# A two-layer graph network with seven-product matmuls: an output sum in halves, two output products set between the relational ones, and a new order in the fill and the first turn

## The chip, the cores and the metric

The kernel runs on one core of a Trainium2 chip. A core has five engines with instruction streams of their own: TensorE (PE) for matmuls and transpositions, VectorE (DVE), ScalarE (ACT), GpSimd (POOL) and SyncE (SP), which here only issues transfers. The metric is the device time of one execution in microseconds (us), the median of several runs. Everything is computed in 32-bit floats.

## The reference, cut to what matters

64 graphs of 256 nodes with 256 features each go through two layers. Layer 0 is a graph attention (GAT) twice, a norm, a feed-forward with ReLU (256 to 1024 and back), and a norm. Layer 1 is a relational attention with 8 heads and 4 relations, a norm, a feed-forward with GELU, and a norm.

```python
def _gat(h, adj, W, a, out_features):
    Wh = h @ W                                    # 256 -> 256
    e = leaky_relu(Wh @ a[:out] + swapaxes(Wh @ a[out:], 1, 2), 0.2)
    att = softmax(where(adj > 0, e, NEG), axis=1)
    return att @ Wh
# layer 0
h = _gat(_gat(x, adj, W1, a1), adj, W2, a2)
h = _layernorm(x + h, g_ln1, b_ln1)
x = _layernorm(h + relu(h @ w_ff1 + b_ff1) @ w_ff2 + b_ff2, g_ln2, b_ln2)
# layer 1
q, k = heads(x @ Wq + bq), heads(x @ Wk + bk)     # 8 heads of 32
attn = softmax(q @ k.T / sqrt(32))
out = sum(attn * (adj == r) @ heads(x @ Wv[r] + bv[r]) for r in range(4))
x = _ln(x + out @ Wo + bo, g1, beta1)
return _ln(x + gelu(x @ W1 + b1) @ W2 + b2, g2, beta2)
```

## The kernel before

**Groups and turns.** The 64 graphs are cut into 32 groups (`NG`) of two; a group is T = 4 blocks of 128 nodes, two to a graph. A fill (L539 to L567 and L1694 to L1853) brings in the weights and does all of layer 0 for group 0 but its end, and the two GATs of group 1. Then come 32 calls of `turn(y_, x_, z)`. A turn works on three groups at once: layer 1 of group y_, the feed-forward of layer 0 of group x_ = y_ + 1, and both GATs of group z = y_ + 2. The first 30 turns have a group z (in the code: `if Z`). In their order a turn has: the projections q and v of the relational attention and the first product of layer 0's feed-forward; the scores, exponentials, masks and weighted sums of the 8 heads; then the stretch that the change touches in every turn: the product with Wo (`out_(0)` and `out_(1)`, one for each graph), the second product of layer 0's feed-forward, between its parts the GAT of group z; then layer 1's feed-forward.

**Products in seven.** The large products are computed as two by two blocks with 7 products instead of 8 (Strassen and Winograd's form), so the inputs of some products are sums or differences of quarters, formed on DVE. `HiddenOut` (L1016) is the second product of a feed-forward. Its four sums take the quarters of the hidden layer `h`: sums 1 and 2 go into a tile called `eq` in the profile, sums 3 and 4 into `eaq`:

```python
o, x_, y_, op = ((s1, a21, a22, ALU.add), (s2, s1, a11, ALU.subtract),
                 (s3, a11, a21, ALU.subtract), (s4, a12, s2, ALU.subtract))[n - 1]
```

A sum is one instruction over 128 x 1024 elements. A product is 8 matmuls, which are 16 records in the profile. Products 1 and 2 read `h` (`yf<-wf,h`), 5 and 6 read sums 1 and 2 (`yf<-wf2t,eq`), 3 and 7 read sums 4 and 3 (`yf<-wf,eaq`), 4 reads `h`. `add(n)` adds what a product has left in its PSUM bank to the rows y. Products 1, 2 and 5 start in banks of their own; 6, 7 and 4 go on in the bank of 1, and 3 in that of 5, each after the add of the product before it there. `out(1)` is `product(1)` and then `add(1)`. The differences of weights that the form needs (`w2t` for layer 1's second product; `wvm`, `w1m`, `w2m` in the code) are formed once, on POOL, by `made(ops, n)`, n instructions a call (L631).

**Banks.** Most products write into a ring of six PSUM banks (`bank(...)`): a product can start when the bank's reader of before has ended. So a late reader on DVE or ACT holds PE.

**The order.** In the fill the order of all engines is that of the code. In the turns PE, SP, DVE and ACT follow the code in the first part and PE and SP in all of it; the rest is ordered by a planner. `with behind(mark)` puts an instruction behind another.

**The stretch in the middle of a turn.** In a turn with a group z its order before is this (L1507 to L1600):

```python
out.sums(1)                      # DVE, eq
shares(1)                        # DVE: zo transposed (L1174), division of po
out_(0)                          # PE: yop, then DVE: the add to y
mv = moments(y_, 2, y, range(NB))
out.sums(2)                      # DVE, eq
out_(1)
...
out(1)                           # PE: product 1, DVE: add 1
```

After it come the scores of the GAT (L819 is its leaky ReLU, on DVE), sum 4, `offsets` (DVE, `nm`, L896), products 2 and 5, and then 6, 3 and 7, with the `hpp` matmuls of the GAT's first sums between them. `norm` is moments on DVE and two instructions on POOL (`rs`, L888 and L889); `offsets` and `applied_norm` need its result.

**The fill.** `gat_weights` transposes the GAT's weights and the first x; `to_features` (L536) copies the two transposed banks of x, one on ACT and one on DVE. After the weights' small products (`gwep`) the adjacency of group 0 is squared on ACT as a check of its values (`checked`), copied and transposed on PE (`aTp`, L755), and then `project(0, [0, 1])` makes the products `xpp` (L773).

**The first projections.** The first turn starts with the end of the fill: `rest()` is `second_half` (L1848). There the second half of group 0's rows is transposed into `h2T`, whose two parts are copied from their banks. `Projections` (L1065) then makes q and v in steps 1 to 7, with four differences on DVE (`p.sums()`), and copies each bank of q on ACT (L1101) and adds v's on DVE.

Of the kernel before, what the change touches and what calls it, by code (L numbers as in the profile page):

```python
# [16 lines left out]
P = 128  # L17
# [368 lines left out]
def narrow_path(  # L386
# [152 lines left out]
    def gat_weights():  # L539

        w1s = work.tile([P, KB, F], F32, tag="hT", name="gw1")
        nc.scalar.dma_start(w1s, g_W1.rearrange("(c p) f -> p c f", p=P))
        w2e = work.tile([P, KB, WX], F32, tag="wh", name="gw2e")
        nc.sync.dma_start(w2e[:, :, :F], g_W2.rearrange("(c p) f -> p c f", p=P))
        load_first(0)
        gcols = columns([v.rearrange("f o -> (f o)") for v in (g_a1, g_a2)], "ga", nc.scalar, "yt")

        def transposed(w, name):
            wt = work.tile([P, KB, F], F32, tag="e", name=f"{name}t")
            for c in range(KB):  # L550
                ps = bank(f"{name}tp{c}")
                for k in range(KB):
                    nc.tensor.transpose(ps[:, k * P:(k + 1) * P], w[:, k, c * P:(c + 1) * P], ident)
                nc.vector.tensor_copy(wt[:, c, :], ps[:, :F])
            return wt

        w1t, w2t = transposed(w1s, "gw1"), transposed(w2e, "gw2")
        a1, a2 = gcols()
        g[0]["xT"] = to_features(g[0]["y"], "xT0")
        for k in range(KB):  # L560
            ps = bank(f"gwap{k}")
            for c in range(KB):
# [150 lines left out]
    def normed_features(u, l, xn, natural=False, copied=(), later=False):  # L713
# [17 lines left out]
        for q in range(Q):  # L731
            for a in range(Q):
                to, at = hT[q * 32:(q + 1) * 32, a], yt[a * 32:(a + 1) * 32, q]
                if q == a:
                    nc.gpsimd.tensor_copy(to, at)  # L735
                else:
                    if n not in copied:
                        nc.sync.dma_start(to, at)
                    elif later:
                        moves.append((to, at))  # L740
                    else:
                        nc.scalar.copy(to, at)
                    n += 1
# [272 lines left out]
    class HiddenOut:  # L1016
# [6 lines left out]
            s.a = [h1[:, k * K2:(k + 1) * K2, b * N:(b + 1) * N] for b in range(2) for k in range(2)]  # L1023
            s.ps = {}

        def sums(s, *which):
            a11, a12, a21, a22 = s.a
            s1, s2, s3, s4 = s.s
            for n in which:
                o, x_, y_, op = ((s1, a21, a22, ALU.add), (s2, s1, a11, ALU.subtract),  # L1030
                                 (s3, a11, a21, ALU.subtract), (s4, a12, s2, ALU.subtract))[n - 1]
                mark["quarters"] = nc.vector.tensor_tensor(o, x_, y_, op)  # L1032

        def product(s, n):
            b11, b21, b22, t1, t2, t3, t4 = s.w
            K2, F2 = FB // 2, F // 2
            if n in (1, 2, 5):
                s.ps[n] = bank(f"yf{n}_{s.n}")
            for old, new in ((1, 6), (6, 7), (7, 4), (5, 3)):
                if n == new:  # L1040
                    s.ps[n] = s.ps[old]
            a, w_ = {1: (s.a[0], b11), 2: (s.a[1], b21), 5: (s.s[0], t1), 6: (s.s[1], t2),
                     3: (s.s[3], b22), 7: (s.s[2], t3), 4: (s.a[3], t4)}[n]
            for i in range(NB):
                for k in range(K2):
                    nc.tensor.matmul(s.ps[n][:, i * F2:(i + 1) * F2], a[:, k, i * P:(i + 1) * P], w_[:, k, :],  # L1046
                                     start=n in (1, 2, 5) and i == 0 and k == 0, stop=True,
                                     skip_group_check=True)
# [16 lines left out]
    class Projections:  # L1065
# [7 lines left out]
            s.h = [[hT[k][:, b * N:(b + 1) * N] for b in range(G)] for k in range(KB)]  # L1073
            s.one, s.two, s.begun, s.t = {}, {}, set(), [None] * 4

        def sums(s):
            tt = work.tile([P, HPB, NB * N], F32, tag="e", name=f"tq{s.u}").rearrange("p a n -> p (a n)")
            s.t = [tt[:, n * N:(n + 1) * N] for n in range(4)]
            for n, (x_, y_) in enumerate(((s.h[0][1], s.h[0][0]), (s.h[1][1], s.t[0]),
                                          (s.h[1][1], s.h[0][1]), (s.h[1][0], s.t[1]))):  # L1080
                nc.vector.tensor_tensor(s.t[n], x_, y_, ALU.subtract)

        def out(s, x, o, b):
            if x == "q":
# [240 lines left out]
    def turn(y_, x_, z, rest=None):  # L1325
# [49 lines left out]
        with order:  # L1375
            if not y_:
                p("q1 v1")
                rest()
                p("q2 v2")
            p.sums()  # L1380
            if X:
                n = X.pop("n")
                if y_:
                    offsets(*n)
                if y_:
                    p("q2 v2 q1 v1")
                else:
                    offsets(*n)
                applied_norm(X["y"], *n, [0, 1, 2, 3])
                p("q5")  # L1390
            else:
# [9 lines left out]
                w, wy = waiting[0]  # L1401
                last = moments(w, 3, wy, range(NB))
            if X:
                moved(moves, 2)
                p("q6")
                moved(moves, 1)
                p("v6")
                moved(moves, 3)
                times(X["y"], rg1)
                p("q3 q7 v7")  # L1410
# [96 lines left out]
            if X:  # L1507
                out = HiddenOut(x_, 0, X["y"], X["h1"], wf2s, out_sums(x_, 0))
                if Z:
                    out.sums(1)  # L1510
            if Z:
                shares(1)
            if not y_:
                with behind("low"):
                    made(w1m, 2)
                    made(w2m, 4)
            out_(0)
            if Z:
                mv = moments(y_, 2, y, range(NB))
# [1 line left out]
                n = norm(y_, 2, y, range(NB))  # L1521
            piece()
            if Z:
                out.sums(2)
            elif X:
                out.sums(1)
                out(1, 2)
# [9 lines left out]
                applied_norm(y, *n)  # L1537
                n = norm(y_, 2, y, range(NB, T))
            if Z:
                out(1)  # L1540
                Z["m"].scores(0)
                Z["m"].scores(1)
                Z["m"].exp(0)
# [31 lines left out]
            if Z:  # L1575
                out.product(6)
                hT = normed_features(y_, 2, y, copied=(1, 2, 4, 5, 7, 8, 10, 11))
                nc.scalar.activation(work.tile([P, 1], F32, tag="ve", name=f"ve{y_}"), mhalf[:, 0:1], AF.Gelu)
                out.add(6)
                out.sums(3)  # L1580
# [113 lines left out]
    with tc.manual_schedule(engines={getattr(mybir.EngineType, n) for n in  # L1694
# [202 lines left out]
```

## Time and profile before

| | |
|---|---|
| median of 3 runs | 2943.12 us (2942.83 to 2954.23) |
| the profiled execution | 2942.66 us |
| its span in the profile | 2941.0 us |
| TensorE clock granted, mean | 0.998 |
| PE busy | 2913.7 us (99%) |
| DVE busy | 2631.4 us (89%) |
| ACT busy | 1907.9 us (65%) |
| POOL busy | 707.9 us (24%) |
| from yop to yop, in the middle of the run | 89.77 us |

The span is the time from the first to the last instruction in the trace of one execution. A line of a timeline gives start, duration, engine, line of the code, operation, output<-input, shape and count, and in brackets an idle time before it with what ended it. The ends of matmuls are modelled, so that the duration of a group of matmuls is longer than the distance to the start of the next group. A group of a page's fifth part has the busy time, the mean of one in ns, and the idle time before.

### The profile page before, as it was taken

Reading aid. Unit: us, or ns where it says so; the run is one execution under the profiler, and the core shown is the slowest. Engines: PE = TensorE matmul, PEld = TensorE weight load, DVE = VectorE, ACT = ScalarE, POOL = GpSimd, SP = SyncE. Lnnn points to the kernel's source line nnn. Section 1 sums busy time; section 2 is a strip of 40 time slices with the busy share of each in tenths; the row PEclk is TensorE's granted clock in tenths of the full one; section 3 lists DMA queues with packets and bytes.
Section 4 is the critical chain, followed back from the end, with each engine's and each line's share of the span. In section 5 each row is a group of like instructions: output and inputs, shape, how many; then the busy total and the mean of one; then the engine's idle time right before and its main releaser. Section 6 shows DMA issues by size and latency. Waiting matters only on the chain.

```text
span 2941.0 us, 58470 instructions
## 1 busy us (share of the span) xinstructions
PE 2913.7 (99%) x21966; PEld 2477.7 (84%) x21966; DVE 2631.4 (89%) x5087; ACT 1907.9 (65%) x3985; POOL 707.9 (24%) x931
## 2 busy tenths in 40 slices
PE   9999999999999999999999999999999999999998
PEld 7788888888888888888888888888888888888876
DVE  5889999899989999999999899999999998999987
ACT  5576676676666766766766666667667666666653
POOL 3322221222221222212222212222122222222210
PEclk9999999999999999999999999999999999999999
DMA  5011211111111212111111111121112121121000
GB/s 153 15 36 40 44 37 34 38 42 41 42 36 27 43 40 44 38 34 37 43 40 42 36 27 43 40 44 37 36 35 43 39 44 35 28 42 40 24 10 16
DMA packets 417860, 115.11 MB, mean 39 GB/s; under 512 B 359994, under 2 KB 409380, under 8 KB 417572
## 3 DMA queue, kind: packets, MB, share of 16 engines
q1 hardware_dynamic: 416172, 109.98, 16.5%
q8 instruction: 176, 2.88, 0.4%
q0 software_dynamic: 1056, 1.05, 0.1%
q14 instruction: 112, 0.92, 0.1%
q10 hardware_dynamic: 344, 0.28, 0.0%
HBM read 72.51 MB, written 16.90 MB: 30 GB/s over the span
## 4 chain that ended last, share of the span: by engine, by line
PE 96%; DVE 2%; ACT 1%; POOL 1%; DMA 0%; issue 0%; POOLq 0%; DVEq 0%; ACTq 0%
PE yf L1046 27%; PE h1a L954 15%; PE h1b L954 12%; PE po L1163 8%; PE v L1114 6%; PE qk L1114 6%; PE sp L1135 4%; PE hpp L851 4%; PE ygp L862 4%; PE xpp L773 4%; PE yop L862 4%; PE zo L1166 2%; DMA first<-in_adj_dram 0%; ACT h L972 0%; POOL w2t L631 0%
## 5 line engine op out<-in xcount | busy, mean ns | idle before, releaser
L1144 ACT ACTIVATE e<-sp 128x512 f32<-128x512 f32 x512 | 270.9, 612 | 71.2 <-issue 43.7
L1148 DVE TENSOR_TENSOR ea<-e,aT 128x1024 f32<-128x1024 f32 x256 | 310.7, 1215 | 1.6 <-ACT e L1144 1.6
L963 DVE TENSOR_TENSOR h<-h1a,h 128x512 f32<-128x512 f32 x293 | 201.7, 689 | 90.3 <-PE h1a L954 89.1
L906 ACT ACTIVATE y<-y,nm,rs 128x256 f32<-128x256 f32 x442 | 235.0, 591 | 58.1 <-DVE nm L896 57.4
L735 POOL COPY hT<-yt 32x256 f32<-32x256 f32 x244 | 211.4, 866 | 144.7 <-PE v L1114 90.9
L966 ACT COPY h<-h1b 128x512 f32<-128x512 f32 x293 | 175.4, 599 | 109.0 <-PE h1b L954 107.2
L888 POOL TENSOR_SCALAR rs<-mv 128x4 f32<-128x4 f32 (+1 forms) x134 | 41.2, 307 | 794.6 <-DVE mv L878 625.4
L972 ACT ACTIVATE h<-h,cols 128x256 f32<-128x256 f32 x512 | 226.1, 504 | 9.8 <-DVE h L963 9.6
L1101 ACT COPY qk<-qk 128x512 f32<-128x512 f32 x128 | 74.3, 580 | 232.5 <-PE qk L1114 230.0
L1176 POOL TENSOR_TENSOR low<-low,rq 128x16 f32<-128x16 f32 x64 | 13.9, 217 | 844.0 <-DVE rq L1175 836.2
L877 DVE BATCH_NORM_STATS2 st<-y 128x6 f32<-128x256 f32 x512 | 208.3, 408 | 4.6
L972 ACT ACTIVATE h<-h1a,cols 128x256 f32<-128x256 f32 x256 | 103.0, 467 | 142.3 <-PE h1a L954 142.2
L1054 DVE TENSOR_TENSOR y<-yf,y 128x256 f32<-128x256 f32 x448 | 182.3, 407 | 11.3 <-PE yf L1046 11.3
L918 DVE TENSOR_TENSOR y<-y,rb 128x1024 f32<-128x1024 f32 x126 | 163.3, 1296 | 3.2
L727 POOL COPY hT<-yt 32x256 f32<-32x256 f32 x120 | 124.9, 1041 | 145.2 <-PE h1a L954 136.2
L1153 DVE TENSOR_TENSOR es<-e 128x1024 f32<-128x1024 f32 x128 | 155.6, 1216 | 0.0
L915 DVE TENSOR_TENSOR y<-y,rg 128x1024 f32<-128x1024 f32 x126 | 152.8, 1213 | 0.0
L889 POOL TENSOR_TENSOR rs<-rs,mhalf 128x4 f32<-128x4 f32 (+1 forms) x134 | 148.2, 1106 | 8.3
L822 ACT ACTIVATE s<-s 128x512 f32<-128x512 f32 x128 | 76.4, 627 | 109.8 <-DVE s L819 109.4
L1135 PE MATMUL sp<-qk 32*128 32x256 f32 x2048 | 138.4, 394 | 0.0
L954 PE MATMUL h1a<-tt,wf 128*128 128x256 f32 x512 | 137.7, 392 | 0.0
L1046 PEld LDWEIGHTS yf<-wf,eaq 128*128 128x128 f32 x1024 | 120.2, 193 | 20.3 <-DVE eaq L1032 11.9
(290 smaller groups left out, 7849.0 us busy)
## 6 DMA issues: line engine op xcount, KB each, us to landing
hT<-yt SPq DMA_DIRECT2D x666, 32.0 KB, 1.9
y<-in_x_dram SPq DMA_DIRECT2D x32, 512.0 KB, 4.3
xq<-in_x_dram SPq DMA_DIRECT2D x240, 64.0 KB, 2.1
aq<-in_adj_dram SPq DMA_DIRECT2D x240, 64.0 KB, 2.3
rows<-line SPq DMA_DIRECT2D x60, 256.0 KB, 3.2
out_dram<-y SPq DMA_DIRECT2D x30, 512.0 KB, 2.8
wf<-in_L_gnn_w_ff_dram SPq DMA_DIRECT2D x2, 1024.0 KB, 8.3
w<-in_L_gnn_W_dram SPq DMA_DIRECT2D x2, 1024.0 KB
```

What stands on the lines that cost most here:

```text
L735: nc.gpsimd.tensor_copy(to, at)
L862: nc.tensor.matmul(ps[:, i * F:(i + 1) * F], lhs(t, k), rhs(b, k), start=(k == 0), stop=(k == n - 1))
L877: nc.vector.bn_stats(st[:, t, :], y[:, t, :])
L906: mark["normed"] = nc.scalar.activation(y[:, t, :], y[:, t, :], AF.Identity, bias=nm[:, t:t + 1], scale=rs[:, t:t + 1])
L954: nc.tensor.matmul(ps[:, i * N:(i + 1) * N], w_[:, f * P:(f + 1) * P], m, start=first and i == 0, stop=True, skip_group_check=True)
L972: nc.scalar.activation(y, y if ps is None else ps[:, i * N:(i + 1) * N], func, bias=bi[:, f:f + 1])
L1046: nc.tensor.matmul(s.ps[n][:, i * F2:(i + 1) * F2], a[:, k, i * P:(i + 1) * P], w_[:, k, :], start=n in (1, 2, 5) and i == 0 and k == 0, s ...
L1114: nc.tensor.matmul(ps[:, i * N:(i + 1) * N], l, r, start=n in (1, 2, 5) and i == 0, stop=True, skip_group_check=True)
L1135: nc.tensor.matmul(ps[a][:, j * N:(j + 1) * N], k_[hp, m, j0:j0 + P], q[hp, m, b * N:(b + 1) * N], start=True, stop=True)
L1144: nc.scalar.activation(e[:, a, :], ps[a], AF.Exp, scale=isd)
L1148: nc.vector.tensor_tensor(ea[:, a:a + 2, :], e[:, a:a + 2, :], ab[:, None, :].to_broadcast([P, 2, NB * N]), ALU.mult)
L1163: nc.tensor.matmul(po[hp, m * N:(m + 1) * N], vs[:, hp], w[:, a, j * N:(j + 1) * N], start=(n == 0), stop=(n == len(terms) - 1))
```

## The change

- In the fill both copies of the first transposed x are on DVE; `project(0, [0, 1])` stands before the check of the adjacency and its transposition.
- In group 0's first output, sum 4 and products 2 and 5 stand before the GAT's scores and exponentials; products 3 and 7 and the norm stand before `made(wvm, 4)`, POOL's differences of the v weights.
- `second_half` transposes first, copies one part on DVE and one on ACT, takes the first difference of the projections, sets the row of ones on DVE instead of POOL, and only then takes the rest of the moments and the norm; `offsets` stands before the other three differences. In the first turn the copy of q6 stands before two moves on ACT, not behind them.
- In the first turn two of the four differences `w2m` are put behind the copies of the transposed y in POOL's order (`mark["turned"]`), not in front of them.
- In all turns with a group z, sum 2 is formed in two halves, the first before `shares(1)`, the second where the whole stood; and the first two of the eight matmuls of product 1 stand between `out_(0)` and `out_(1)`.

```diff
@@ gat_weights
-        g[0]["xT"] = to_features(g[0]["y"], "xT0")
+        g[0]["xT"] = to_features(g[0]["y"], "xT0", (nc.vector.tensor_copy,) * 2)
@@ normed_features
-                    nc.gpsimd.tensor_copy(to, at)
+                    mark["turned"] = nc.gpsimd.tensor_copy(to, at)
@@ HiddenOut
-        def sums(s, *which):
-            a11, a12, a21, a22 = s.a
-            s1, s2, s3, s4 = s.s
+        def sums(s, *which, half=None):
+            K2 = FB // 2
+            part = slice(0, K2) if half is None else slice(half * K2 // 2, (half + 1) * K2 // 2)
+            a11, a12, a21, a22 = [a[:, part] for a in s.a]
+            s1, s2, s3, s4 = [a[:, part] for a in s.s]
...
-        def product(s, n):
+        def product(s, n, some=None):
...
-            if n in (1, 2, 5):
+            if n in (1, 2, 5) and n not in s.ps:
                 s.ps[n] = bank(f"yf{n}_{s.n}")
...
-            for i in range(NB):
-                for k in range(K2):
-                    nc.tensor.matmul(...)
+            steps = [(i, k) for i in range(NB) for k in range(K2)]
+            for i, k in steps if some is None else steps[some]:
+                nc.tensor.matmul(...)
@@ Projections
-        def sums(s):
+        def sums(s, which=range(4)):
...
-                nc.vector.tensor_tensor(s.t[n], x_, y_, ALU.subtract)
+                if n in which:
+                    nc.vector.tensor_tensor(s.t[n], x_, y_, ALU.subtract)
@@ turn
             if not y_:
                 p("q1 v1")
-                rest()
+                rest(lambda: p.sums([0]))
                 p("q2 v2")
-            p.sums()
+                offsets(*X["n"])
+                p.sums([1, 2, 3])
+            else:
+                p.sums()
...
             if X:
-                moved(moves, 2)
+                if y_:
+                    moved(moves, 2)
                 p("q6")
-                moved(moves, 1)
+                moved(moves, 1 if y_ else 2)
                 p("v6")
+                if not y_:
+                    moved(moves, 1)
                 moved(moves, 3)
...
                 if Z:
                     out.sums(1)
+                    out.sums(2, half=0)
             if Z:
                 shares(1)
             if not y_:
                 with behind("low"):
                     made(w1m, 2)
-                    made(w2m, 4)
+                    made(w2m, 2)
             out_(0)
...
             if Z:
-                out.sums(2)
+                out.sums(2, half=1)
+                out.product(1, slice(0, 2))
...
             out_(1)
...
             if Z:
-                out(1)
+                out.product(1, slice(2, None))
+                out.add(1)
...
             if Z:
                 out.product(6)
                 hT = normed_features(y_, 2, y, copied=(1, 2, 4, 5, 7, 8, 10, 11))
+                if not y_:
+                    with behind("turned"):
+                        made(w2m, 2)
@@ fill
+        project(0, [0, 1])
         checked(0, g[0]["aq"], squares[:, 2:4].rearrange("p a n -> p (a n)"))
         turn_a = early_adjacency_of(0, 0)
         turn_a()
-        project(0, [0, 1])
...
         first.sums(1)
         first(1)
         first.sums(2)
+        first.sums(4)
+        first(2, 5)
         spread(b["m"])
         powers(b["m"])
-        first.sums(4)
-        first(2, 5)
         b["m"].masks(0)
...
+        first(3)
+        first(7)
+        n0 = norm(0, 1, a["y"], range(NB))
         made(wvm, 4)
-        first(3)
-        n0 = norm(0, 1, a["y"], range(NB))
-        first(7)
...
             nc.scalar.copy(h2T[:, 1, ns], ph[1][:, ns])
             nc.gpsimd.memset(h2T[one, KB - 1, ns], 1.0)
-            (nc.scalar.copy, nc.vector.tensor_copy)[b_](h2T[:, 0, ns], ph[0][:, ns])
+            nc.scalar.copy(h2T[:, 0, ns], ph[0][:, ns])
...
-        def second_half():
+        def second_half(first_difference):
+            turned(a["y"], "h2T0", range(NB, T), ph)
+            ns = slice(N, 2 * N)
+            nc.vector.tensor_copy(h2T[:, 0, ns], ph[0][:, ns])
+            nc.scalar.copy(h2T[:, 1, ns], ph[1][:, ns])
+            first_difference()
+            nc.vector.memset(h2T[one, KB - 1, ns], 1.0)
             b["n"] = norm(1, 0, b["y"], mv=mv)
-            turned(a["y"], "h2T0", range(NB, T), ph)
-            half(1)
```

More of the change, by code (lines that the diff above doesn't have):

```diff
@@ L1043, in product @@
                      3: (s.s[3], b22), 7: (s.s[2], t3), 4: (s.a[3], t4)}[n]
-            for i in range(NB):
-                for k in range(K2):
-                    nc.tensor.matmul(s.ps[n][:, i * F2:(i + 1) * F2], a[:, k, i * P:(i + 1) * P], w_[:, k, :],
-                                     start=n in (1, 2, 5) and i == 0 and k == 0, stop=True,
-                                     skip_group_check=True)
+            steps = [(i, k) for i in range(NB) for k in range(K2)]
+            for i, k in steps if some is None else steps[some]:
+                nc.tensor.matmul(s.ps[n][:, i * F2:(i + 1) * F2], a[:, k, i * P:(i + 1) * P], w_[:, k, :],
+                                 start=n in (1, 2, 5) and i == 0 and k == 0, stop=True,
+                                 skip_group_check=True)
         def add(s, n):
@@ L1074, in __init__ @@
             s.one, s.two, s.begun, s.t = {}, {}, set(), [None] * 4
-        def sums(s):
-            tt = work.tile([P, HPB, NB * N], F32, tag="e", name=f"tq{s.u}").rearrange("p a n -> p (a n)")
-            s.t = [tt[:, n * N:(n + 1) * N] for n in range(4)]
+        def sums(s, which=range(4)):
+            if which[0] == 0:
+                tt = work.tile([P, HPB, NB * N], F32, tag="e", name=f"tq{s.u}").rearrange("p a n -> p (a n)")
+                s.t = [tt[:, n * N:(n + 1) * N] for n in range(4)]
             for n, (x_, y_) in enumerate(((s.h[0][1], s.h[0][0]), (s.h[1][1], s.t[0]),
                                           (s.h[1][1], s.h[0][1]), (s.h[1][0], s.t[1]))):
-                nc.vector.tensor_tensor(s.t[n], x_, y_, ALU.subtract)
+                if n in which:
+                    nc.vector.tensor_tensor(s.t[n], x_, y_, ALU.subtract)
         def out(s, x, o, b):
@@ L1386, in turn @@
                     p("q2 v2 q1 v1")
-                else:
-                    offsets(*n)
                 applied_norm(X["y"], *n, [0, 1, 2, 3])
```

## The prediction

> **What bounds the kernel now.** I read the page first, then the waits of the PE, then the timelines of PE, DVE, ACT and POOL in four places (fill, first projections, end of the first turn, end of a later turn), then the windows with the granted clock. The busy line of the page, and the two longest lines of the waits of the PE:
>
> ```profile
> PE 2913.7 (99%) x21966; PEld 2477.7 (84%) x21966; DVE 2631.4 (89%) x5087; ACT 1907.9 (65%) x3985; POOL 707.9 (24%) x931
> ...
> PE yf L1046 <- DVE y L1054: 4.5, 6, 2.6
> PE aTp L755 <- ACT xT L536: 3.8, 1, 3.8
> ```
>
> PE sets the time, and idles only 27 us of 2941. But busy is not fast: a wait that is shorter than the tail of the matmul before it shows no idle time, only a later start. So I read starts. Timeline of the PE at the end of the sixth turn (start, duration, ..., count):
>
> ```profile
> 583.28 3.75 PE L862 MATMUL yop<-wo,qk 128*128 128x256 f32 x16
> 586.88 3.73 PE L1046 MATMUL yf<-wf,h 128*128 128x128 f32 x32
> 590.45 3.74 PE L1046 MATMUL yf<-wf2t,eq 128*128 128x128 f32 x32
> 594.15 2.05 PE L1046 MATMUL yf<-wf,eaq 128*128 128x128 f32 x16
> 596.04 1.91 PE L851 MATMUL hpp<-xp,s 128*128 128x258 f32 x8
> 597.95 2.05 PE L1046 MATMUL yf<-wf,eaq 128*128 128x128 f32 x16
> 599.84 1.91 PE L851 MATMUL hpp<-xp,s 128*128 128x258 f32 x8
> ```
>
> Start to start, undisturbed: 32 yf take 3.57 (586.88 to 590.45), so 16 take 1.79; 8 hpp take 1.74 (599.84 to 601.58), and 8 ygp in the fill 1.73, so 16 yop should take 3.46. Seen: yop 3.60 (0.14 over), products 5 and 6 3.70 (0.13 over, the wait of product 3), product 3 1.89 (0.10), hpp 1.91 (0.17, the wait of product 7), product 7 1.89 (0.10). That is 0.64 us a turn, in 29 like turns after the first 18.6 us. Who is late is seen in the DVE's timeline:
>
> ```profile
> 580.60 1.18 DVE L1032 TENSOR_TENSOR eq<-h 128x1024 f32<-128x1024 f32 x1
> 582.45 0.72 DVE L1174 STREAM_TRANSPOSE rz<-zo 128x512 f32<-128x512 f32 x1 [0.67 <-PE zo L1166]
> ...
> 587.03 1.19 DVE L1032 TENSOR_TENSOR eq<-eq,h 128x1024 f32<-128x1024 f32 x1
> ...
> 593.68 0.41 DVE L1054 TENSOR_TENSOR y<-yf,y 128x256 f32<-128x256 f32 x1
> ...
> 596.54 1.36 DVE L1032 TENSOR_TENSOR eaq<-h 128x1024 f32<-128x1024 f32 x1
> ```
>
> After 0.67 idle at 582.45 and 0.28 at 585.21 (for yop) DVE runs without a gap over 0.04 to 597.90. Add 5 ends at 594.09 and product 3, which goes into the same bank, starts at 594.15; sum 3 ends at 597.90 and product 7 starts at 597.95.
>
> **Steady turns.** Half of sum 2 goes into the 0.67. A 512-wide half is between the 256-wide subtraction (0.42, L932) and the 1024-wide one (1.19): on their line 0.68. Neighbours overlap by 0.08 (580.60 + 1.18 against the next starts), so it takes 0.60 of the 0.67 and the transposition of zo starts where it did. The other half leaves at 587.03 a pitch of 0.60 where 1.11 stood (587.03 to 588.14): everything to sum 3 is 0.51 earlier, as nothing in that run waits otherwise: rs on POOL is done at 591.82 and used at 592.59, the exponentials at 592.20 and used at 593.00, the last norm at 594.85 and its transposition starts behind three others. The two matmuls of product 1 (4 of its 16 records, 0.45) move in front of the second yop; their total is the same. The second yop waited for the division (584.93) with 0.14; it now starts at 583.28 + 1.73 + 0.45 = 585.46 and waits for nothing. Behind it the DVE's add of it would come at 587.4, when the half sum has just ended (587.63). Product 7: the PE alone would gain the 0.14 + 0.13 + 0.10 + 0.17 = 0.54 before it, DVE allows 0.51. I take 0.51 x 29 = 14.8 us. What is late next: sum 3 again, at about the same instant as the PE. Bounds: 0.30 (DVE run shortened, but ACT's scaled xp hold hpp) to 0.64 a turn, 8.7 to 18.6.
>
> **End of the first turn.** The same place, with POOL's lines first, then DVE's:
>
> ```profile
> 138.04 1.72 POOL L631 TENSOR_TENSOR w2t<-w,w2t 128x512 f32<-128x512 f32 x1
> 139.74 0.67 POOL L888 TENSOR_SCALAR rs<-mv 128x4 f32<-128x4 f32 x1
> 140.49 1.85 POOL L889 TENSOR_TENSOR rs<-rs,mhalf 128x4 f32<-128x4 f32 x1
> ```
>
> ```profile
> 137.74 2.57 DVE L819 SCALAR_TENSOR_TENSOR s<-s 128x512 f32<-128x512 f32 x2
> ...
> 142.37 0.16 DVE L896 SCALAR_TENSOR_TENSOR nm<-mv,rs 128x4 f32<-128x4 f32 x1 [0.92 <-POOL rs L889]
> ```
>
> POOL's six weight differences delay rs by 2.9 us (the last two, 136.81 to 139.76), and DVE's pair of L819 takes 2.57 beside them against 1.28 in a later turn. Product 3 could start at 137.61 + 3.57 = 141.18 and starts at 143.95: 2.77. Then the clock falls:
>
> ```profile
> 11.50:14.90 3.40, 0.80 (x6) 0.77 (x7) 0.00 (x0) 2.64 (x5) 0.00 (x0) 1.00 0.75 202
> 14.90:18.30 3.40, 3.27 (x9) 2.00 (x7) 0.09 (x1) 1.18 (x3) 0.00 (x0) 0.50 1.06 334
> ...
> 141.20:144.60 3.40, 0.80 (x7) 0.65 (x6) 2.46 (x12) 2.03 (x4) 1.14 (x1) 1.00 0.00 0
> 144.60:148.00 3.40, 3.40 (x16) 3.21 (x15) 3.38 (x8) 3.15 (x9) 1.89 (x4) 0.50 0.04 10
> ```
>
> (Second column PE busy, third from last the clock.) A window with 0.80 busy is followed by one at 0.50: product 3 takes 2.99 (1.20 over), hpp 2.29 (0.55 over). In all 4.52. With the two differences behind the transpositions POOL is free at 136.84, rs is done near 138.5, and DVE runs in the steady pitches: half sum to 134.96 (slowed as the 1.52 at 134.19), add and moments 1.80, add 1 0.31, L819 1.21, sum 4 1.13, nm 0.07, add 2 0.34, masks 0.68, add 5 0.41: 140.91, before the PE (141.04). Product 7 then waits for sum 3 about 0.2. Gain 4.4, bounds 3.3 to 4.6. The moved pair is in no hurry: it now stands behind POOL's four copies, some 2.6 us beside DVE work that had 3.18 idle at 151.21; its first reader is the second output sum, later in the turn.
>
> The Trainium skill (TensorE: Matmul & The Clock Gate, why this matters for your kernels) counsels "No PE-idle gaps >~3µs". The 2.60 of idle at 143.95 is below that and the row shows 0.50 all the same; by the rule the 1.75 of slow matmuls would not be this gap's doing and the gain here would be 2.7, by the row it is 4.4.
>
> **Fill.** aTp (14.10) waits 3.76: its bank is freed by ACT's copy of xT (13.48), behind the table load (11.04 to 12.32) and the square (12.34 to 13.48), which wait for the adjacency that lands 9.5 us after 1.50. With both copies on DVE, gw2e's two small copies are 0.61 later (pitch 7.51 to 8.12), so gwep starts at 8.93, not 8.32; its last copy ends 2.49 later, at 11.42; 8 xpp at full clock 1.75 (16 in 3.50 at 33.41), 4 aTp 0.44: colsp at 13.65, not 17.87. Gain 4.2. The table load has no wait any more in the changed order and falls into ACT's empty stretch from 7.92. Square now stands behind two copies of xp, and behind it aT, which DVE reads only at the masks, 8 us later. Costs that could show: colsp needs the columns, issued last at 7.64; the nearest landing times are 2.8 (128 KB) and 11.1, so 10.4 or 18.7; I take the first, as these are 4 KB. Bounds 0 to 4.6.
>
> **First output and projections of the first turn.** First(2, 5) before the scores: DVE's list before add 6 holds the same operations, and product 7 waits for add 6: 0, within 0.2. Wvm behind the norm on POOL: rs 0.3 earlier, the next rs about 0.8 later (84.1, behind 3.0 us of wvm, against 83.26), with nm and the adds behind it in DVE's queue; ACT's norms then end near 86.45, where the PE comes at 86.3: 0, within 0.3. In the second half DVE copies at 87.00, subtracts, sets the ones (0.31 on POOL, at most that here), and only then takes the moments (1.17) that stood before: the add that frees product 5's bank ends at 89.95, so 5 starts at 90.0 as it did (90.08). But nm comes at 90.85 instead of 91.30, and ACT copies q6 at once instead of after two moves (0.82): at 94.45, not 95.85. The waits before q3 (0.28) and q7 (0.72) go; v7 waits for v6's copy (95.85) and starts at 95.9, not 96.95. 1.0, bounds 0 to 1.3.
>
> **Sum.** 14.8 + 4.4 + 4.2 + 0 + 1.0 = 24.4 us. The profiled execution took 2942.66 (span 2941.0 and 1.7 around it), 0.46 under the median of 2943.12: 2918.3.
>
> **Rivals.** (a) The half sum does not pay: the pitch of the half is nearer to 1.11 (fixed cost) and zo's transposition starts that much later. For it: the slot is only 0.07 wider than the half. Against: the 256-wide rows. Then 9.6 is left: 2933.1; 0.12. (b) The fill stays held, by columns landing at 18.7 or by a clock that falls after gwep (now about 1.2 idle in the window 8.1 to 11.5, where 1.2 was idle before): 2922.5; 0.07. (c) Slower: the second yop now takes another bank and has a new wait for ACT in the changed order. If the read that frees it is ACT's h (ends 584.32) it costs nothing at 585.46; were it the score rows (L811, end 587.50) it would cost 2.0 in each of 29 turns, with nothing of the 0.51: 2942.7 + 58 - 9.6 = 2991; it decides from 585.3 on. Against: those are issued after it. 0.04.
>
> **Numbers.** My case has 0.77, its own range 2914 to 2926. The predicted time is its own. The range 2912 to 2931 takes in (b) and most of the way to (a). About 0.5% (14.7 us) is what a measurement here can tell from no change: below 2928.4 lie my case and (b), 0.84; (a) is no change, 0.12; (c) 0.04.
>
> **What would show it.** Right: turns of 89.26 instead of 89.77 (yop to yop), sum 2 in two pieces of about 0.68 with the first before the transposition of zo, no 0.50 clock after 5 us, aTp without idle, nm of the first turn without POOL's wait. Wrong: yop to yop at 89.7 or more, idle before the second yop, or a new first idle on ACT in the fill.

## The result, and the profile after

| | before | after |
|---|---|---|
| median, runs beside each other | 2945.69 us (6 runs) | 2918.66 us (6 runs, 2917.95 to 2921.20) |
| ratio | | 0.9904 (95% interval 0.9888 to 0.9920) |
| the profiled execution | 2942.66 us, span 2941.0 | 2917.95 us, span 2916.3 |
| yop to yop, in the middle of the run | 89.77 us | 89.23 us |

The change is faster by 1.0%. Two of the six runs before took 2953.42 and 2954.23 us, so that the medians are 27.0 us apart and the spans of the two profiled executions 24.7. The busy line of the page after:

```profile
PE 2895.0 (99%) x21966; PEld 2474.8 (85%) x21966; DVE 2634.0 (90%) x5119; ACT 1907.7 (65%) x3984; POOL 706.9 (24%) x930
```

The page shows hardly anything: PE is at 99% as before and DVE is no less busy. In the waits of the PE the line of aTp is gone, and that of yf for DVE fell from 4.5 us in 6 waits to 2.4 in 4. The rest is again in the starts. Timeline of the PE at the end of the sixth turn, after (start, duration, ..., count):

```profile
571.76 1.89 PE L862 MATMUL yop<-wo,qk 128*128 128x256 f32 x8
573.49 0.61 PE L1048 MATMUL yf<-wf,h 128*128 128x128 f32 x4
573.94 1.89 PE L862 MATMUL yop<-wo,qk 128*128 128x256 f32 x8
...
582.36 1.95 PE L1048 MATMUL yf<-wf,eaq 128*128 128x128 f32 x16
584.15 1.91 PE L851 MATMUL hpp<-xp,s 128*128 128x258 f32 x8
585.89 2.05 PE L1048 MATMUL yf<-wf,eaq 128*128 128x128 f32 x16
587.78 1.91 PE L851 MATMUL hpp<-xp,s 128*128 128x258 f32 x8
```

The first yop, the two matmuls of product 1 and product 3 (582.36 to 584.15) take their own 1.73, 0.45 and 1.79, and so do the first hpp, 1.74 (584.15 to 585.89). Only product 7 takes 1.89 instead of 1.79 (585.89 to 587.78). Who still holds it is in the timeline of DVE:

```profile
570.30 0.69 DVE L1034 TENSOR_TENSOR eq<-eq,h 128x512 f32<-128x512 f32 x1
570.93 0.72 DVE L1178 STREAM_TRANSPOSE rz<-zo 128x512 f32<-128x512 f32 x1
...
575.51 0.66 DVE L1034 TENSOR_TENSOR eq<-eq,h 128x512 f32<-128x512 f32 x1
576.08 0.68 DVE L865 TENSOR_TENSOR y<-yop,y 128x512 f32<-128x512 f32 x1
...
584.48 1.36 DVE L1034 TENSOR_TENSOR eaq<-h 128x1024 f32<-128x1024 f32 x1
```

The first half fills the idle place in front of the transposition. The second leaves a pitch of 0.57 where 1.11 stood. Sum 3 ends at 585.84 and product 7 starts at 585.89, as late as the hpp let it, but its weights are sum 3, which ended only 0.05 before. That loading them late costs the 0.10 that is left is tested below.

The fill, timeline of PE before and then after. `colsp` is the transposition of small parameter columns, the first group of PE behind the part that the change orders anew:

```profile
14.10 0.66 PE L755 MATMUL aTp<-ident,first 128*128 128x128 f32 x4 [3.76 <-ACT xT L536]
14.59 3.34 PE L773 MATMUL xpp<-gwe,xT 128*128 128x260 f32 x8
17.87 0.30 PE L500 MATMUL colsp<-ident,colsr 28*128 28x28 f32 x1
```

```profile
10.37 2.27 PE L773 MATMUL xpp<-gwe,xT 128*128 128x260 f32 x8
...
13.00 0.24 PE L500 MATMUL colsp<-ident,colsr 28*128 28x28 f32 x1
```

The end of the first turn: timeline of PE before, of PE after, and of POOL after:

```profile
143.95 3.19 PE L1046 MATMUL yf<-wf,eaq 128*128 128x128 f32 x16 [2.60 <-DVE y L1054]
```

```profile
135.95 2.05 PE L1048 MATMUL yf<-wf,eaq 128*128 128x128 f32 x16
```

```profile
129.55 1.60 POOL L631 TENSOR_TENSOR w2t<-w,w2t 128x512 f32<-128x512 f32 x1
131.98 0.24 POOL L888 TENSOR_SCALAR rs<-mv 128x4 f32<-128x4 f32 x1 [0.83 <-DVE mv L878]
```

aTp waits for nothing and colsp comes at 13.00 instead of 17.87. In the first turn rs waits for the moments and no longer stands behind weight differences; product 3 starts at 135.95, without an idle time of PE, and takes 1.89 up to the next, not 2.99. Where the time came from, by the starts of the same instructions in both traces (`ygp`: the last sums of group 1's second GAT in the fill, one for each graph; `yop`: the product with Wo):

| part | read from | predicted | measured |
|---|---|---|---|
| fill | colsp, 17.87 and 13.00 | 4.2 | 4.9 |
| first output | second ygp, 83.12 and 78.73: 4.39, less the 4.87 | 0 | -0.5 |
| projections of the first turn | first yop, 130.45 and 125.30: 5.15, less the 4.39 | 1.0 | 0.8 |
| first turn | first to second yop, 93.78 and 89.55 | 4.4 | 4.2 |
| other turns | second to last yop, 2667.19 and 2651.93 | 14.8 | 15.3 |
| behind the last yop | 49.58 and 49.52 | 0 | 0.1 |
| sum | spans | 24.4 | 24.7 |

### The profile page after: what moved, and what is told of

It reads as the page before. It is cut to its first block, busy times and chain, and to the rows that moved or that the text cites. A ratio compares the mean times of both kernels' runs of the same rounds, so it can differ in the third digit from the quotient of the medians.

```text
span 2916.3 us, 58469 instructions
## 1 busy us (share of the span) xinstructions
PE 2895.0 (99%) x21966; PEld 2474.8 (85%) x21966; DVE 2634.0 (90%) x5119; ACT 1907.7 (65%) x3984; POOL 706.9 (24%) x930
## 4 chain that ended last, share of the span: by engine, by line
PE 97%; DVE 2%; ACT 1%; POOL 0%; issue 0%; POOLq 0%; DVEq 0%
PE yf L1048 27%; PE h1a L954 15%; PE h1b L954 12%; PE po L1167 8%; PE v L1118 7%; PE qk L1118 6%; PE sp L1139 5%; PE hpp L851 4%; PE ygp L862 4%; PE xpp L773 4%; PE yop L862 4%; PE zo L1170 2%; ACT h L972 0%; DVE h L963 0%; PE idle L584 0%
## 5 line engine op out<-in xcount | busy, mean ns | idle before, releaser
L1167 PE MATMUL po<-e,v 128*32 128x256 f32 x2048 | 135.5, 382 | 0.0
```

The costliest lines, as they stand in the source:

```text
L1167: nc.tensor.matmul(po[hp, m * N:(m + 1) * N], vs[:, hp], w[:, a, j * N:(j + 1) * N], start=(n == 0), stop=(n == len(terms) - 1))
```

## The experiments

**The two parts of the steady turns, each alone.** The first has only the halves, the second only the split of product 1:

```diff
                 if Z:
                     out.sums(1)
+                    out.sums(2, half=0)
...
-                out.sums(2)
+                out.sums(2, half=1)
```

> The kernel before, with sum 2 in two halves and nothing else. My theory: DVE's run becomes 0.54 us shorter, but the second yop still waits 0.14 for the division, which is not touched. So 0.13 (product 3) + 0.10 + 0.17 (product 7) = 0.40 goes, and the distance from yop to yop falls from 89.77 to 89.37 us. Rival (the half sum does not pay): 89.7 or more.

```diff
+            if Z:
+                out.product(1, slice(0, 2))
             out_(1)
...
-                out(1)
+                out.product(1, slice(2, None))
+                out.add(1)
```

> The kernel before, with two matmuls of product 1 between the two yop, and nothing else. My theory: the second yop waits no longer (0.14), but DVE's run is as long as before, and product 7 still waits for its end: the 0.14 turns up as a longer wait of products 3 and 7, and yop to yop stays at 89.77. Rival (each wait of PE is worth its own time): 89.63.

Measured, yop to yop: 89.27 with the halves, 89.77 with the split. The split alone does exactly nothing. The timeline of its PE shows why:

```profile
599.91 3.74 PE L1046 MATMUL yf<-wf2t,eq 128*128 128x128 f32 x32
603.76 2.05 PE L1046 MATMUL yf<-wf,eaq 128*128 128x128 f32 x16
```

The 0.14 gained at the second yop returns as a longer wait of products 3 and 7: products 5 and 6 now take 3.85 (599.91 to 603.76) where they took 3.70. PE can only arrive earlier at a place where DVE is late. The halves alone gave 0.50, not 0.40: I had left out that with the yop still waiting 0.14, product 7's weights come in time, and its 0.10 goes too. Timelines of PE and of DVE with the halves alone:

```profile
595.26 1.95 PE L1048 MATMUL yf<-wf,eaq 128*128 128x128 f32 x16
597.05 1.91 PE L851 MATMUL hpp<-xp,s 128*128 128x258 f32 x8
```

```profile
593.71 1.36 DVE L1034 TENSOR_TENSOR eaq<-h 128x1024 f32<-128x1024 f32 x1
```

Sum 3 ends at 595.07, 0.19 before product 7, and product 7 takes 1.79. With both parts the yop's 0.14 is gone and the 0.10 is back. So of the 0.54 a turn the halves alone give 0.50, and the split adds 0.04 to them.

**The whole sum in the idle place.** The changed kernel, with sum 2 undivided before `shares(1)`:

```diff
-                    out.sums(2, half=0)
+                    out.sums(2)
...
-                out.sums(2, half=1)
```

> The changed kernel, with the whole of sum 2 (not only its first half) before the transposition of zo. My theory: the 1.13 of sum 2 does not fit into the 0.67 that DVE had idle, so the division for the second graph ends 0.5 us later, at about the instant at which the second yop starts, which the two matmuls of product 1 ahead of it just cover; PE loses at most 0.1 there, DVE's run to sum 3 is 0.1 shorter, and yop to yop is 89.1 to 89.3 us, against 89.23. Rival (the second yop has no such room): 89.5 or more.

Measured: 89.32, just above the 89.1 to 89.3 expected. The two lines of PE that carry it:

```profile
575.39 1.97 PE L862 MATMUL yop<-wo,qk 128*128 128x256 f32 x8
...
587.42 1.95 PE L1048 MATMUL yf<-wf,eaq 128*128 128x128 f32 x16
```

The second yop comes 0.56 behind the matmuls of product 1 instead of 0.45, and takes 1.81 instead of 1.72: 0.20 lost to the late division, where at most 0.1 was expected. Product 7 (587.42 to 589.21) takes its own 1.79: the 0.10 is gained. 89.23 + 0.20 - 0.10 = 89.33. So the whole sum is too long for the idle place, and the half fits.

**The fill, each part alone.**

```diff
-        g[0]["xT"] = to_features(g[0]["y"], "xT0")
+        g[0]["xT"] = to_features(g[0]["y"], "xT0", (nc.vector.tensor_copy,) * 2)
```

> The kernel before, with both copies of the first transposed x on DVE, and nothing else: aTp still stands before the products xpp. My theory: the bank of aTp is free early, aTp starts when the adjacency has landed (about 11.1 us), and colsp comes at 13.3 instead of 17.87; the window from 14.9 has a full clock. This part alone gives nearly all of the fill. Rival (both parts are needed): colsp at 16 or later.

```diff
+        project(0, [0, 1])
         checked(0, g[0]["aq"], squares[:, 2:4].rearrange("p a n -> p (a n)"))
         turn_a = early_adjacency_of(0, 0)
         turn_a()
-        project(0, [0, 1])
```

> The kernel before, with the products xpp before the adjacency's check and transposition, and one copy of the transposed x still on ACT. My theory: ACT's table load waits for nothing any more and the copy on ACT ends near 9.8 us, so xpp starts at 10.2 and colsp at about 12.8, a little before the 13.00 of the whole change, since DVE has one copy less ahead of gwep. Rival (both parts are needed): colsp at 16 or later.

colsp came at 13.54 and at 13.79. The first weights land some tenths earlier or later in each execution, so the distance from the first transposition of x (xT0p) to colsp says more: 11.49 before, 6.90 with the copies alone, 6.43 with the order alone, 6.71 with both (6.29 to 13.00). Counted the same way, 6.9 and 6.4 were expected for the parts, and the rival, that both are needed, falls. Either part alone removes the wait for ACT's copy, since either one takes it out from behind the square. The second copy on DVE even costs time beside the new order: the five profiled executions with both parts have 6.71 to 6.86, 0.28 to 0.43 more than the one with the order alone. The kernel with the order alone lost 1.6 of it again (66.23 from colsp to the first h2T0p, against 64.62 before), in a window of slow clock (0.50) from 16.91 to 20.33; in the window ahead of it PE had been busy for 3.13 of 3.41 us, in part with products of one column.

**The two weight differences.** The kernel before with two of them moved, and with one:

```diff
-                    made(w2m, 4)
+                    made(w2m, 2)      # 3 in the second kernel
...
+                if not y_:
+                    with behind("turned"):
+                        made(w2m, 2)  # 1 in the second kernel
```

> The kernel before, with the last two of the four differences w2m of the first turn behind POOL's copies of the transposed y, and nothing else. My theory: POOL's rs comes 2.9 us earlier, product 3 waits 0.2 us at most instead of 2.60, the window that had a clock of 0.50 has 1.00, and the first distance from yop to yop falls from 93.78 to about 90.1 us (89.77 and the 0.3 that the changed kernel's first turn also has over its others). Rival (the clock falls there for another cause): 91.8 or more.

> The kernel before, with only the last one of the four differences w2m moved. My theory: rs comes 1.7 us earlier, product 3 still waits about 1 us, but the idle time is too short a part of its window to bring the clock down: 1.00 in all windows, and the first distance from yop to yop is about 91 us. Rival (any idle time of that kind brings the clock down, or its cause is another): a window at 0.50 again, and 92.1 or more.

The first distance from yop to yop was 90.09 with two and 90.40 with one; before it was 93.78. Neither has a slow window there. With two, the size is the predicted one (product 3 waited 0.46, more than the 0.2, presumably as DVE's run here has the whole sum 2 in it). With one, PE was idle for 0.59 before product 3 and not for about 1: rs came at 136.92, 7.69 behind the first yop, where before it came 9.29 behind it (139.74 and 130.45), 1.60 sooner, but the 1.85 of the second step on POOL also shrank to 1.31.

**What the clock took.** The expectation of both had the slow window as a sure price of an idle time of 2.6. It is not. The kernel with the copies alone keeps that wait of product 3, 2.59 in its first turn, and has no slow window; its first distance is 92.39, as is that of the kernel with the order alone, so the slow clock was 1.39 of the 93.78. The windows of the clock lie on a grid of 3.41 us: in the trace before, slow ones start at 14.92 and 144.63, which is 38.0 windows. The grid starts at another instant in each execution. With the copies alone the wait lies half in one window and half in the next (behind the length of the window PE's busy time; third from last the clock):

```profile
134.92:138.33 3.41, 2.03 (x19) 1.84 (x17) 2.49 (x4) 0.81 (x2) 2.92 (x3) 1.00 0.00 0
138.33:141.74 3.41, 2.20 (x18) 2.18 (x19) 3.38 (x16) 3.22 (x8) 0.20 (x1) 1.00 0.00 0
```

In the kernel with the split alone most of the wait in the fill, which ends at 14.34, lies in one window, and the clock is slow from 13.62 to 37.51, seven windows, of which the first is shown:

```profile
10.21:13.62 3.41, 1.17 (x6) 0.67 (x4) 0.86 (x2) 2.33 (x2) 0.00 (x0) 1.00 0.92 231
13.62:17.03 3.41, 2.69 (x9) 2.29 (x10) 0.00 (x0) 1.25 (x4) 0.00 (x0) 0.50 0.87 277
```

That stretch costs much more: from colsp to the first h2T0p it took 73.30 us, against 64.62 in the profiled execution of before. If the wait is what does it, filling the wait with matmuls must take both prices away and leave the order as it is:

```diff
-            for c in range(KB):
+            for c in list(range(KB)) * (1 + 3 * k):
                 nc.tensor.matmul(ps[:, :WX], w1t[:, c, k * P:(k + 1) * P], w2e[:, c, :],
                                  start=(c == 0), stop=(c == KB - 1))
```

> The kernel before, with the matmuls of the second gwep done four times over (2.6 us more of them, results the same), so that PE works through most of the time in which it waits for the copy of xT; no other order or wait is changed. My theory: the start of aTp stays at about 14.1, but no window of the fill has a clock of 0.50: colsp at about 16.3 instead of 17.87. And the two kinds of times of the kernel before, 2941 to 2946 and 2953 to 2954, come from whether that idle time brings the clock down for one window of 3.4 us or for seven (23.9 us, seen in two of the runs above), so that none of these five is above 2947. Rival (the long ones come from elsewhere): one or two of the five at 2953 or more.

```profile
14.11 0.66 PE L755 MATMUL aTp<-ident,first 128*128 128x128 f32 x4
14.60 1.92 PE L773 MATMUL xpp<-gwe,xT 128*128 128x260 f32 x8
16.45 0.24 PE L500 MATMUL colsp<-ident,colsr 28*128 28x28 f32 x1
```

aTp started at 14.11 and colsp came at 16.45, with a full clock. All 12 executions took 2941.42 to 2943.88 us. Of 17 executions of the kernel before on the same chip 13 took 2941.02 to 2944.93, and four 2952.12 to 2954.34. None of 12 against four of 17 could still be chance. But over all runs the long executions (some 10 us above the others of their kernel) are 10 of the 41 in which the wait stands, and none of the 33 in which it is gone or filled; and in both long ones that were profiled the seven slow windows follow that wait. So the long ones come from it; work that is thrown away removes them. The median stays (2943.20 and 2943.65); how many of the executions without a trace had a single slow window there is not known.

**The first output undone.** The changed kernel with this part in the order of before:

```diff
-        first.sums(4)
-        first(2, 5)
         spread(b["m"])
         powers(b["m"])
+        first.sums(4)
+        first(2, 5)
...
+        made(wvm, 4)
         first(3)
-        first(7)
         n0 = norm(0, 1, a["y"], range(NB))
-        made(wvm, 4)
+        first(7)
```

> The changed kernel, with the order of group 0's first output as before (scores and exponentials ahead of sum 4 and products 2 and 5; the four wvm ahead of product 3 and the norm). My theory: in the new order sum 4 follows sum 2, which it reads, and the masks follow the exponentials with nothing between, which makes add 6 0.36 us later; and nm runs beside wvm on POOL (0.68 instead of 0.16). Undone, the first yop comes at 124.8 instead of 125.30. Rival (the 0.5 is a difference from run to run, or belongs to the fill): 125.2 to 125.4.

The first yop came at 125.75, and colsp 0.94 later than in the changed kernel (13.94 and 13.00). From colsp to the first yop it is 111.81, against 112.30 in the changed kernel (and 112.33 in its second profile): 0.5, as expected. The places are product 7 and nm. In the kernel before, timeline of the PE, then of DVE:

```profile
76.24 2.02 PE L1046 MATMUL yf<-wf,eaq 128*128 128x128 f32 x16 [0.20 <-DVE y L1054]
```

```profile
81.40 0.16 DVE L896 SCALAR_TENSOR_TENSOR nm<-mv,rs 128x2 f32<-128x2 f32 x1 [2.58 <-POOL rs L889]
```

In the changed kernel:

```profile
71.71 2.02 PE L1048 MATMUL yf<-wf,eaq 128*128 128x128 f32 x16 [1.20 <-DVE y L1056]
```

```profile
76.49 0.68 DVE L896 SCALAR_TENSOR_TENSOR nm<-mv,rs 128x2 f32<-128x2 f32 x1 [1.22 <-POOL rs L889]
```

Product 7 waited 0.20 before and 1.20 now. Of that, 0.6 is only moved here from product 3, which came 0.50 late before and lost 0.10 with its weights; the rest is that DVE needs 8.22 from sum 1 to the end of add 6 (63.34 to 71.56) where it needed 7.85 (68.25 to 76.10). The same instruction nm took 0.16 with POOL idle and 0.68 with a subtraction on POOL (76.43 to 77.15); the norm on ACT and the transposition behind it then made PE 0.23 later.

**The projections alone.** The kernel before with the new `second_half`, the early `offsets` and the order of ACT's moves:

```diff
-                rest()
+                rest(lambda: p.sums([0]))
                 p("q2 v2")
...
+                if y_:
+                    moved(moves, 2)
                 p("q6")
...
```

> The kernel before, with only the new order of the second half, of the offsets and of ACT's moves in the first turn. My theory: from the second h2T0p to the projections' end it gains what the changed kernel gains there, 0.76 us: no wait of q3, q7 waits for nothing, v7 0.3 for the copy of v6, and the first yop at 129.7 instead of 130.45. Rival (it pays only with the rest of the change): 130.3 or more.

Its fill had seven slow windows too, so that the first yop came at 139.21 and not at 129.7. From the first h2T0p (91.99) to it are 47.22; before they were 47.96 (82.49 to 130.45): 0.74, as expected, and it does not need the rest of the change.

**A better version.** Two edits on the changed kernel: sum 3 in two halves, and the first output with scores first and `made(wvm, 3)` in the time in which POOL waits.

```diff
                 out.add(6)
-                out.sums(3)
+                out.sums(3, half=0)
+                out.sums(3, half=1)
                 out(3)
...
+        made(wvm, 3)
         first(3)
         first(7)
         n0 = norm(0, 1, a["y"], range(NB))
-        made(wvm, 4)
...
         n1 = norm(0, 1, a["y"], range(NB, T))
+        made(wvm, 1)
```

> The changed kernel with two edits. First, sum 3 of the turns with a group z in two halves, one right after the other: product 7's first weights wait for the first half only. Second, group 0's first output with scores and exponentials ahead of sum 4 and products 2 and 5 again, three of the four wvm in the time in which POOL waits for the moments and one after the second norm. My theory: in the changed kernel product 7 starts at its own time but its first weight load comes late behind sum 3 (0.10 between its first two matmuls), so yop to yop falls from 89.23 to 89.13 us, 2.9 us in 29 turns; the first output gives 0.5; the median is 3 to 4 us below that of the changed kernel. Rival (the 0.10 is a fixed price of that change of weights, or the extra instruction delays what follows on DVE): 89.23 or more, and a difference under 1 us.

> The changed kernel again, on the same chip as the one above, as its measure. My theory: its median is between 2917 and 2922 us, no run of it is 10 us above the others, since nothing in its fill waits long enough, and yop to yop is 89.23. Rival (the long fills are hidden by chance so far): one of its runs above 2927.

| | median | all | ratio to before |
|---|---|---|---|
| changed kernel | 2919.42 us | 2918.79 to 2921.79 (6) | 0.9914 (0.9899 to 0.9928) |
| better version | 2916.61 us | 2914.23 to 2916.79 (5) | 0.9899 (0.9883 to 0.9915) |

```profile
585.53 1.95 PE L1048 MATMUL yf<-wf,eaq 128*128 128x128 f32 x16
587.31 1.91 PE L851 MATMUL hpp<-xp,s 128*128 128x258 f32 x8
```

yop to yop is 89.12, and product 7 takes its own 1.78 (585.53 to 587.31): the 0.10 was the price of weights that came late. No run of the changed kernel was long, as expected. From colsp to the first yop it is 111.50 against 112.33. The medians are 2.8 apart, a little less than the 3 to 4 expected, and the two sets of times do not overlap; the two intervals do, so that the size of the difference rests on the traces (29 x 0.11 + 0.83 = 4.0), from which a later fill (colsp at 14.04 and 13.55) takes 0.5 and a slow window at 2880 some 1.7 in the two profiled executions (spans 2915.2 and 2917.1).

## Why the prediction was right

The time was 2918.66, predicted 2918.3. The main case held, but not each of its steps.

- **Steady turns: right.** The half has 0.69 and 0.66 us (0.68 predicted), fits the idle place, and the transposition starts as it did. I took the 0.51 that DVE was to give and not the 0.64 of all waits; it gave 0.54. That sum 3 and PE would come at about the same instant was also right, and is why 0.10 stayed.
- **The weight of the split: not seen.** The prediction credits the whole change of the place with one sum. The runs with one part each show that the split is worth nothing alone and 0.04 of 0.54 beside the halves; what it does is to start the second yop late enough for the division.
- **First turn: 4.2 of 4.4.** The order is right (product 7 waits 0.17 for sum 3, about 0.2 predicted). But the 1.2 and 0.55 of slow matmuls were counted as a sure gain. Of these 1.75 the clock had 1.39, and only in executions in which its grid falls so; in another one the same change of order would have found 1.4 less to gain.
- **Fill: the term was mis-sized and its upper bound, 4.6, too low.** Two steps: the copies on DVE put gwep at 8.51 and not at 8.93, because the first copy starts when its own bank is ready (7.11, not 7.51); and xpp starts at 10.37 on the first half of gwe, not at 11.42 when both are done; it then takes 2.10 up to aTp and not 1.75. In sum 0.65 earlier: 13.00 for 13.65. Some of the first step is this execution's own: from xT0p to gwep it has 2.22, four others with both parts 2.25 to 2.37, and the prediction 2.55. The columns had landed by then, as assumed. Here too a slow window was counted as a sure gain: the kernel before with one w2m moved has the fill of before and no slow window in it, and needs 9.88 from xT0p to colsp instead of 11.49, 1.6 less.
- **First output: "0, within 0.2" was wrong,** it cost 0.5. I argued that the list of DVE before add 6 holds the same operations. It does, in a worse order: sum 4 now follows sum 2, which it reads (1.32 from start to start, where the step from sum 2 to the scores took 1.13), and the first mask follows the scores at once and waits for ACT's exponentials (0.17 more). And nm beside POOL was not counted.
- **Projections: 0.8 of 1.0.** The two waits that were named show no idle time any more; by the starts they were 0.45 and 0.97, and 0.16 and 0.11 are left. The one of v7 has the cause named, ACT's copy of v6 (0.32 of wait). That copy ends 0.28 later than reckoned, because nm comes 0.13 later and the norms, q5, v5, q6 and two moves follow it on ACT.
- **Rivals.** (a) falls by the 0.66 of the half; (b) by colsp at 13.00, with the clock at 1.00 throughout the fill; (c) by the second yop, which starts with no wait 0.45 behind the matmuls before it.

Fill and first output were off by 0.7 and 0.5 in opposite directions; the near agreement of the sum is partly that, and so partly luck. It is luck too that the execution from which the prediction subtracts had one slow window in the fill and one in the first turn: some 3.0 of the 24.7 us (1.6 and 1.4) are the clock's, and an execution with seven windows or none would have given another sum.

On the clock the Trainium skill (TensorE: Matmul & The Clock Gate, Part 1: The HAM clock gate) describes a free-running window of about 3.4 us and an idle window as what slows the array. The grid of 3.41 agrees with the first; for the second, a window with 1.38 of 3.41 busy (first turn of the kernel with the halves alone) was followed by 0.50 here, so that it need not be idle throughout.

## What to carry to other kernels

When an engine shows no idle time, read starts: a wait shorter than the tail of the work before it is a later start and nothing else, and 0.1 here and there was 15 us in 29 turns. Find the chain that is late at several of these places; shortening that chain paid here at all of them together, while clearing one place on the waiting engine only moved the wait to the next. A wait of PE of 2 us or more had a second price here that depends on the execution, so look at several executions before counting it as gain or as noise.

## What was not expected of the hardware

**The clock's grid.** Windows of 3.41 us whose start differs between executions decide whether a wait costs a slow window. In the traces here, for waits of PE in the fill and the first turn: PE busy for 0.82, 1.01, 1.17 and 1.38 us of a window, then 0.50 in the next; busy for 1.46, 1.80, 2.03 and 2.20, then 1.00. The clearest case is one that no run touched. In all 14 traces PE waits the same 2.40 us behind the last yop, for the differences `tt` of the last feed-forward. In nine of them a window at this wait has 1.00 to 1.16 us busy, the next one has 0.50, and 51.1 to 51.5 us pass from the last yop to the end. In the other five the wait lies across two windows, the emptier of which has 1.72 to 2.11 busy; the clock stays, and the end takes 49.5 to 49.8 us. So the same wait costs some 1.7 us or nothing, by the grid alone, with the old order and with the new. In the fill and the first turn a slow stretch lasted one window (3.41 us) or seven (23.89, in two executions); what decides between them stays open. So does the slow window that followed one with 3.13 us busy, in the stretch with products of one column: in the second trace of the changed kernel a window with the same 3.13 in that stretch (12.13 to 15.54) was followed by 1.00.

**DVE beside POOL.** A subtraction on POOL makes the DVE instruction beside it longer, and is made longer by it: nm of 128x2 took 0.68 us instead of 0.16, the pair of L819 2.57 instead of 1.28, the second half of sum 2 0.98 instead of 0.66 in the first turn, and POOL's own subtraction 2.14 instead of 1.27. The ends look like waiting in turn more than like sharing: nm ends at 77.17 and the subtraction at 77.15, and in the better version at 80.76 and 80.74. The sums on DVE that read PSUM and the statistics with one input kept their times beside the same subtractions (0.67 and 0.43 at 78.63 and 79.33 in the changed kernel). The Trainium skill (GPSIMD Engine Reference, 1. Specifications) says that GpSimd shares its interfaces to SBUF with VectorE and contends with DVE instructions in a two-port mode or with two inputs in SBUF; the traces agree with the second. nm, small as it is, lost more than three times its own duration.
